# A two-layer decoder on one core: the last batch's causal output, linear cross attention, norm and routing in two parts of 128 queries, with two more expert tiles between them

## The chip, the core and the metric

The kernel runs on one core of one Trainium2 chip. A core has a matrix engine (TensorE, in the profile PE, its weight loads PEld) and four others: VectorE (DVE), ScalarE (ACT), GpSimd (POOL) and SyncE (SP), which here only starts transfers between the chip's main memory and the core's own. Each engine works through its own instructions in the order in which the program gives them, and waits on semaphores for the others and for transfers. Matmul results land in PSUM, which has eight banks. The metric is the time of the whole kernel on the device in microseconds (us).

## The reference

A decoder of two layers, each followed by its norm, in float32: four batches of 256 tokens with 256 channels, and a context of 1601 rows for each batch.

```python
# layer 0                                           16 heads of 16
x = norm(x + sliding_window_attention(x))           # window 64
x = norm(x + attention(q=x, kv=[context, x]))       # one head of 256
x = norm(x + ternary_ffn(x))                        # quantised weights and activations
# layer 1                                           16 heads of 192, 4 of keys
x = norm(x + causal_attention(x))                   # keys and values from a latent of 64, rotary part
x = norm(x + gate(x) * linear_attention(x, context) @ Wo)
x = norm(x + moe(x))                                # 8 experts, the best 2 of each token
```

The linear attention uses a feature map f (x + 1 above zero, exp(x) below), so that a batch needs of its context only the sums f(k) v and f(k) for each head. In the mixture of experts (MoE) a token's two best experts each compute w2(silu(w1 x) * w3 x), and the two are added with the router's weights.

## The kernel before, in words

**The order of work.** No line of the kernel says in which order an engine does its work. The functions of the decoder record operations with what they read and write. The `Loom` (lines 176 to 353) then lays them out like a list scheduler: of all operations that could go next it takes the one that can start first (`weave`, line 301), by a model of costs: a time for each operation on each engine (`Side.cost`, line 386; for matmuls the microseconds given to `piece`, line 240), the delay from one engine to the next (`LAT`, line 182), and a model of the transfers (lines 336 to 338): all of them one after the other at `RATE`, 0.25 MB/us, plus a landing time of 1.6 us. Ties go by a priority (`at_prio`) and the order of recording. What comes out is a fixed program for each engine. At run time the engines wait for real data, in that order. So a change in the model alone can change the order of anything. The profile puts matmuls at L253 (`mm`), transposes on PE at L260 (`turn`), plain transfers at L267, and all work of DVE, ACT and POOL at L382, where it is issued.

**The stages.** Layer 0's sliding-window attention (`l0_attention`, line 652) runs together with the context sums (`context_sums`, line 741; matmuls `wkv,KT` and `kf,V` in the profile, sums kvs) from 0 to about 130 us. It loads xt (a batch's x transposed), the weights wqkv, and for each batch the context KT and V in pieces of up to 1 MB, all through SP's one queue. Batches share two buffers of v (`vs[b % 2]`). A softmax is a maximum (`nm`) on DVE, four exponentials on ACT with their sums, a reciprocal (`rs`) on DVE, and a scaling on DVE or POOL; then PE transposes the result (`ident,at`). `l1_weights` (line 1002) multiplies layer 1's weights into each other; `kr<-wkr,trig` is its first step on DVE and needs the transfers wkr and trig. Layer 0's cross attention, the FFN, and layer 1's attention follow.

**The end.** For each batch b the main loop (lines 1464 to 1475) records layer 1's causal attention (`l1_attention`, line 1052: four groups of four heads, `four`, line 1069; in each first queries 0 to 127 against 128 keys, then queries 128 to 255 against 256, then `P·V` for all of them, `aTa,ctk` and `aTb,ctk`; the output projection w2o in two halves), `l1_cross` (line 1126: qf and the gate by `xt,wqg`, `kvs,qf`, the division that gives o, `wxo`), the norm (`norm`, line 602: statistics on DVE, a power on POOL for rstd, transposes on PE), and `route` (line 1227). `route` writes x to two arrays in main memory, xd and acc, and enters each token with its weight into the list of each of its two experts: four indirect transfers on POOL (`enter`, line 1212). A tile is 128 rows of one expert's list. `tile_table` (line 1287) works out on DVE which tiles there are. `expert_tile` (line 1337) fetches a tile's list entries (SP), gathers its rows xg from xd (POOL, L1349), transposes them, multiplies by w1 and w3 (`w,xgT`), takes Tanh and two products (ACT, DVE), transposes, multiplies by w2 (`w2e,ehT`), and adds the result ey to acc by an indirect transfer on POOL (L1357). Each of these add-ups waits until the one before has landed. After batch 3's cross attention, ahead of its routing, stand 5 early tiles (`EARLY`) that the tokens of batches 0 to 2 fill for certain; 18 (`LATE`) follow when all is routed. At the very end acc is loaded, normalised and stored.

The transfer model, and the last loop:

```python
            if op.size is not None:
                self.free["DMA"] = max(self.free["DMA"], at + us) + op.size / self.RATE
                op.end, op.engine = self.free["DMA"] + op.land, "DMA"
...
        if b == B - 1:
            at_prio(8)
            tab, taken = tile_table(EARLY, None)
            for i in range(EARLY):
                expert_tile(i, tab)
```

Of the kernel before, what the change touches and what calls it, by code (L numbers as in the profile page):

```python
# [175 lines left out]
class Loom:  # L176
# [62 lines left out]
    @contextmanager  # L239
    def piece(self, us, claims=(), ins=(), what=""):  # L240

        self.cur = ([], [], list(ins))
        yield
        fns, outs, ins = self.cur
        self.cur = None
        self.op({"PE": (us, us, lambda: [f() for f in fns])}, outs, ins, claims, what=what)
# [54 lines left out]
    def weave(self):  # L301
# [11 lines left out]
        while left:  # L313
# [22 lines left out]
            if op.size is not None:  # L336
                self.free["DMA"] = max(self.free["DMA"], at + us) + op.size / self.RATE
                op.end, op.engine = self.free["DMA"] + op.land, "DMA"
# [70 lines left out]
def decoder(ctx: ExitStack, tc: tile.TileContext, a: dict, out: bass.AP):  # L409
# [178 lines left out]
    def normalise(x):  # L588
        mv = tiny((P, 2, 2), "mv")
        for t in range(2):  # L590
            st = tiny((P, 6), "st")
            k.vector.bn_stats(st, x[:, t, :])
            k.vector.bn_aggr(mv[:, t, :], st)
        rstd = tiny((P, 2), "rstd")
        k.gpsimd.tensor_scalar(rstd, mv[:, :, 1], 1e-5, None, ALU.add)
        k.gpsimd.tensor_tensor(rstd, rstd, mhalf, ALU.pow)
        for t in range(2):
            k.vector.tensor_scalar(
                x[:, t, :], x[:, t, :], mv[:, t, 0:1], rstd[:, t : t + 1], ALU.subtract, ALU.mult
            )  # L600

    def norm(b, x):

        normalise(x)
        xt = xpool.tile((P, 2, S), F32, "xt")
        ps = bank((P, 2, 2, P))
        for t in range(2):
            with piece(0.22, [xt], what="norm"):
                for c in range(2):
                    turn(ps[:, c, t, :], x[:, t, c * P : (c + 1) * P], ident)  # L610
        evac(xt.rearrange("p c (t q) -> p c t q", t=2), ps)
        X[b], XT[b] = x, xt
# [12 lines left out]
    def project_out(pool, x_new, t, x_old, o, wo, gate=None):  # L625
# [6 lines left out]
        if gate is None:  # L632
            evac(oT, pt)
        else:
            k.vector.scalar_tensor_tensor(oT, gate[:, :, t * P : (t + 1) * P], 1.0, pt, ALU.add, ALU.mult)
# [16 lines left out]
    def l0_attention(b):  # L652
# [11 lines left out]
        for i in range(3):  # L664
            pv = bank((P, D))
            with piece(0.86, what="v"):
                for c in range(2):
                    mm(pv, XT[b][:, c, 64 * i : 64 * i + P], wqkv[:, c, 2 * D :], c == 0, c == 1)
# [65 lines left out]
    def feature_map(pool, dst, ps, n, width, bufs=2):  # L734

        e = pool.tile((P, 512), F32, "fm", bufs=bufs)[:n, :width]
        k.scalar.activation(e, ps, AF.Exp)
# [314 lines left out]
    def l1_attention(b):  # L1052
# [16 lines left out]
        def four(q4):  # L1069

            ps = project_in(XT[b], lambda c, j: m_w[:, c, 2 * q4 + j, :], [qeT], "q")
            evac(qeT[:, 2 * q4 : 2 * q4 + 2, :], ps)
            aT0 = pool.tile((P, 2, 2, S), F32, "aTa")
            aT1 = pool.tile((P, 2, 2, P), F32, "aTb")
            for t in range(2):
# [4 lines left out]
                with piece(0.65 if t == 0 else 1.15, [at, aT0, aT1], what="scores"):  # L1080
# [15 lines left out]
                for kc in range(t + 1):  # L1096
# [4 lines left out]
                    dst = aT0[:, :, :, t * P : (t + 1) * P] if kc == 0 else aT1  # L1101
                    evac(dst, pt.rearrange("p (u i) q -> p u i q", u=2))

            po = bank((P, 2, S))
            with piece(1.42, what="pv"):
                for u in range(2):
                    half = slice(64 * u, 64 * u + 64)
                    mm(po[half], ctk[:, 0, :], aT0[:, u], True, False, skip_group_check=True)
                for u in range(2):
                    half = slice(64 * u, 64 * u + 64)  # L1110
                    mm(po[half, :, P:], ctk[:, 1, :], aT1[:, u], False, True, skip_group_check=True)
            evac(qeT[:, 2 * q4 : 2 * q4 + 2, :], po)

        for q4 in range(4):
            four(q4)
        xn = new_x()
        for t in range(2):
            py = bank((P, D))
            with piece(3.46, [xn], what="out"):
                for i in range(8):  # L1120
                    mm(py, qeT[:, i, t * P : (t + 1) * P], w2o[:, i, :], i == 0, i == 7)
            k.vector.tensor_tensor(xn[:, t, :], py, X[b][:, t, :], ALU.add)
        norm(b, xn)


    def l1_cross(b):
        pool = p5
        qf = pool.tile((P, 2, S), F32, "qf", bufs=1)
        pq = project_in(XT[b], lambda c, j: wqg[:, 0, c, j * P : (j + 1) * P], [qf], "q")
        feature_map(pool, qf.rearrange("p j q -> p (j q)"), pq.rearrange("p j q -> p (j q)"), P, 512, 1)  # L1130

        gate = pool.tile((P, 2, S), F32, "gate", bufs=1)
        pg = project_in(XT[b], lambda c, j: wqg[:, 1, c, j * P : (j + 1) * P], [gate], "gate")
        for j in range(2):
            k.scalar.activation(gate[:, j], pg[:, j], AF.Tanh, bias=bg[:, j : j + 1], scale=0.5)
        xn = new_x()
        for t in range(2):
            pn = bank((P, H, 17))
            o = pool.tile((P, H, 16), F32, "o")
            with piece(0.47, [o], what="kvs"):  # L1140
                for j in range(2):
                    mm(
                        pn[:, 8 * j : 8 * j + 8, :].rearrange("p h e -> p (h e)"),
                        qf[:, j, t * P : (t + 1) * P],
# [9 lines left out]
            project_out(pool, xn, t, X[b], o.rearrange("p h e -> p (h e)"), wxo, gate)  # L1154
        norm(b, xn)
# [8 lines left out]
    EARLY = -(-(2 * 3 * S - NE * (P - 1)) // P)  # L1164
    LATE = 2 * T // P + NE - 1 - EARLY
# [61 lines left out]
    def route(b):  # L1227
        pool = p5
        tokens, ahead, onesb, _, _, nxt = state
        for d in (xd, acc):  # L1230
            k.dma_start(d[b * S : (b + 1) * S, :].rearrange("(t p) d -> p t d", p=P), X[b])
        entry = pool.tile((P, 2, 2, 2), I32, "entry", bufs=B)
        k.vector.tensor_copy(
            entry[:, :, :, 1], tokens[:, 2 * b : 2 * b + 2].unsqueeze(2).to_broadcast([P, 2, 2])
        )
        pl = bank((P, 2, NE))
        with piece(0.83, what="route"):
            for t in range(2):
                for c in range(2):
                    mm(pl[:, t, :], XT[b][:, c, t * P : (t + 1) * P], wg[:, c, :], c == 0, c == 1)  # L1240

        lg = tiny((P, 2, NE), "lg")
        k.scalar.activation(lg, pl, AF.Tanh, scale=1.0 / 30.0)
        k.scalar.activation(lg, lg, AF.Exp, scale=30.0)
        m = tiny((P, 2), "lm")
        k.vector.reduce_sum(m, lg, axis=AX.X)
        k.vector.reciprocal(m, m)
        k.vector.tensor_tensor(lg, lg, m.unsqueeze(2).to_broadcast([P, 2, NE]), ALU.mult)
        top = tiny((P, 2, 8), "top")
        ix = tiny((P, 2, 8), "ix", U32)  # L1250
        for t in range(2):

            k.vector.max(top[:, t, :], lg[:, t, :])
            k.vector.max_index(ix[:, t, :], top[:, t, :], lg[:, t, :])
        ixf = tiny((P, 2, 2), "ixf")
        k.vector.tensor_copy(ixf, ix[:, :, 0:2])
        hot = tiny((P, 2, 2, NE), "hot")
        k.vector.tensor_tensor(
            hot,
            iota8.unsqueeze(1).unsqueeze(1).to_broadcast([P, 2, 2, NE]),  # L1260
            ixf.unsqueeze(3).to_broadcast([P, 2, 2, NE]),
            ALU.is_equal,
        )
        hotb = tiny((P, 2, NE), "hotb", BF16)
# [3 lines left out]
        pr = bank((P, 3, NE))  # L1268
        with piece(0.3, what="rank"):
            mm(pr[:, 0, :], ahead, hotb[:, 0, :], True, True)  # L1270
            mm(pr[:, 1, :], onesb, hotb[:, 0, :], True, False)
            mm(pr[:, 1, :], ahead, hotb[:, 1, :], False, True)
            mm(pr[:, 2, :], onesb, hotb[:, 0, :], True, False)
            mm(pr[:, 2, :], onesb, hotb[:, 1, :], False, True)
        at = tiny((P, 2, 1, NE), "place")
        k.vector.tensor_tensor(at[:, :, 0, :], pr[:, :2, :], nxt.unsqueeze(1).to_broadcast([P, 2, NE]), ALU.add)
        k.vector.tensor_tensor(nxt, nxt, pr[:, 2, :], ALU.add)
        k.vector.tensor_tensor(hot, hot, at.to_broadcast([P, 2, 2, NE]), ALU.mult)
        row = tiny((P, 2, 2), "row")
        k.vector.reduce_sum(row, hot, axis=AX.X)  # L1280
        rowi = tiny((P, 2, 2), "rowi", I32)
        k.vector.tensor_copy(rowi, row)
        for t in range(2):
            for e in range(2):
                enter(rowi[:, t, e : e + 1], entry[:, t, e, :])

    def tile_table(n, taken):


        iotaN, start, nxt = state[3:]  # L1290

        def some(w, tag):
            return p5.tile((P, w), F32, f"{tag}{n}", bufs=1)

        nt = some(NE, "nt")
        k.vector.tensor_scalar(
            nt, nxt, 1.0 / P, -127.0 / 256.0 if taken is None else 127.0 / 256.0, ALU.mult, ALU.add
        )
        k.vector.tensor_scalar(nt, nt, MAGIC, MAGIC, ALU.add, ALU.subtract)
        st = start  # L1300
        if taken is not None:
            st = some(NE + 1, "st")
            k.vector.tensor_copy(st, start)
            k.vector.tensor_tensor(st[:, :NE], st[:, :NE], taken, ALU.add)
# [9 lines left out]
        past = p5.tile((P, n, NE), F32, f"past{n}", bufs=1)  # L1314
# [11 lines left out]
        tab = p5.tile((P, 2, n), I32, f"tab{n}", bufs=1)  # L1326
        k.vector.tensor_scalar(tab[:, 0, :], ex, float(NE - 1), None, ALU.min)
        k.vector.tensor_scalar(tab[:, 1, :], row, float(P), None, ALU.mult)
        if taken is None:

            taken = some(NE, "taken")
            k.vector.tensor_tensor(taken, nt, upto, ALU.subtract)
            k.vector.tensor_scalar(taken, taken, float(n), 0.0, ALU.add, ALU.max)
            k.vector.tensor_tensor(taken, taken, nt, ALU.min)
        return tab, taken

    def expert_tile(i, tab):
# [70 lines left out]
        k.op({"POOL": (1.65, 1.65, add_up)}, [acc], [y, ids], size=0.13, what="add up")  # L1408
# [43 lines left out]
    state = moe_prepare()  # L1452
# [11 lines left out]
    for b in range(B):  # L1464
        at_prio(7, b)
        l1_attention(b)
# [90 lines left out]
```

## Time and profile before

| | |
|---|---|
| time, median of 3 runs | 734.64 us (733.61 to 734.69) |
| profiled execution: time, span | 731.26 us, 729.5 us |
| granted clock of PE, mean over the span | 0.979 |
| PE busy | 672.8 us, 92% |
| DVE, ACT, POOL busy | 438.5 (60%), 302.6 (41%), 158.3 (22%) us |
| bytes moved | 63.39 MB, mean 87 GB/s |

The span is the profiled execution's time from its first to its last instruction; its own time is 1.76 us longer. The profile cuts the span into 40 slices, and gives each engine's busy share of a slice in tenths. `PEclk` is the share of PE's full clock that was granted. A line of the timeline gives the start, the time and the engine of instructions of one kind in a row, their line, what they write and read, how many they were, and in brackets how long the engine stood idle before them and what it waited for. A line of the windows gives, for a stretch, its length, then PE, PEld, DVE, ACT and POOL busy with their instruction counts, then the granted clock, the share of the DMA engines and GB/s. A line on a transfer ends with its size and the time from issue to landing. A float32 matmul shows as two instructions of PE (24 for twelve), a transpose as one.

### The profile page before, as it was taken

To read this page: it belongs to the slowest core of one execution; us is meant where nothing else is said; L and a number is where in the kernel's file an instruction comes from. 1 tells how busy PE (TensorE), PEld (TensorE's weight loads), DVE (VectorE), ACT (ScalarE), POOL (GpSimd) and SP (SyncE) were. 2 spreads that over 40 slices of the span, in tenths; PEclk is the share of its full clock that TensorE was granted. 3 is DMA by queue.
4 is the path that set the end of the run, shared out by engine and by line. 5 is a ranking of instruction groups with operands and counts; after the bars stand their busy time and mean duration, and the time that the engine had idled before them with its cause. 6 is when DMAs were issued, how large, how long until landed. Compare 5 with 4: busy or idle time off the path is not lost.

```text
span 729.5 us, 11204 instructions
## 1 busy us (share of the span) xinstructions
PE 672.8 (92%) x3920; PEld 490.8 (67%) x3920; DVE 438.5 (60%) x1067; ACT 302.6 (41%) x931; POOL 158.3 (22%) x190
## 2 busy tenths in 40 slices
PE   7999999999999999999899999999977959999970
PEld 5778787678867786767676777777654635665640
DVE  4899886334493535665999877887754513333323
ACT  2868664211232224343467765656611202222210
POOL 3220324022100000000121010303122456522232
PEclk9999999999999999999999999999999989999995
DMA  9901212538632230000203900003601143312214
GB/s 307 341 18 59 92 35 87 173 128 273 219 115 91 91 122 1 1 0 1 53 1 115 347 1 30 1 30 62 199 2 37 30 56 90 59 21 23 23 22 123
DMA packets 51819, 63.39 MB, mean 87 GB/s; under 512 B 7758, under 2 KB 41684, under 8 KB 51764
## 3 DMA queue, kind: packets, MB, share of 16 engines
q1 hardware_dynamic: 46836, 56.63, 23.9%
q0 software_dynamic: 4928, 6.05, 5.3%
q8 instruction: 32, 0.52, 0.3%
q14 instruction: 23, 0.19, 0.1%
HBM read 54.05 MB, written 8.61 MB: 86 GB/s over the span
## 4 chain that ended last, share of the span: by engine, by line
PE 73%; DVE 13%; DMA 5%; ACT 4%; issue 2%; POOL 1%; SPq 0%; POOLq 0%; DVEq 0%; ACTq 0%
PE bank L253 65%; PE bank L260 8%; DVE at L382 3%; ACT at L382 3%; DMA acc<-ey,mine 2%; DVE nm L382 2%; DVE x L382 2%; DVE h L382 1%; DVE as L382 1%; DMA lists<-entry,rowi 1%; DMA xg<-xd,mine 1%; DVE st L382 1%; DMA x<-acc 1%; POOL rstd L382 1%; DMA wqkv<-in_wqkvT 0%
## 5 line engine op out<-in xcount | busy, mean ns | idle before, releaser
L382 ACT ACTIVATE at<-at,nm 128x128 f32<-128x128 f32 (+1 forms) x256 | 106.3, 418 | 23.5 <-DVE nm L382 22.9
L253 PE MATMUL bank<-w,xgT 128*128 x184 | 85.0, 608 | 0.5 <-ACT xgT L382 0.5
L260 PE MATMUL bank<-ident,at 128*128 128x128 f32 (+1 forms) x440 | 60.4, 275 | 1.1 <-DVE at L382 0.4
L253 PEld LDWEIGHTS bank<-w,xgT 128*128 128x128 f32 x184 | 35.0, 197 | 37.1 <-issue 36.0
L260 PEld LDWEIGHTS bank<-ident,at 128*128 128x128 f32 (+1 forms) x440 | 50.7, 141 | 13.0 <-issue 4.8
L382 POOL TENSOR_SCALAR rstd<-mv 128x2 f32<-128x2 f32 x24 | 6.3, 263 | 244.2 <-DVE mv L382 226.1
L253 PE MATMUL bank<-V,aT 128*128 128x256 f32 (+1 forms) x240 | 55.2, 380 | 1.4 <-DVE o L382 1.4
L253 PE MATMUL bank<-KT,qT 128*128 128x512 f32 (+1 forms) x128 | 53.8, 554 | 0.0
L253 PEld LDWEIGHTS bank<-V,aT 128*128 128x128 f32 (+1 forms) x240 | 45.0, 190 | 11.6 <-issue 4.4
L1357 POOL DMA_INDIRECT acc<-ey,mine x23 | 36.1, 1569 | 72.7 <-DVE ey L382 42.1
L253 PE MATMUL bank<-kf,V 128*128 128x256 f32 (+1 forms) x208 | 49.9, 382 | 1.1 <-DVE kf L382 1.1
L382 DVE TENSOR_REDUCE nm<-at 128x4 f32<-128x512 f32 x64 | 50.7, 809 | 0.5
L253 PE MATMUL bank<-wkv,KT 128*128 128x256 f32 (+1 forms) x208 | 49.7, 383 | 0.0
L382 ACT ACTIVATION_READ_ACCUMULATOR at<-at,nm 128x1 f32 x256 | 48.4, 189 | 0.0
L253 PE MATMUL bank<-w2e,ehT 128*128 x184 | 43.9, 385 | 2.9 <-ACT ehT L382 2.8
L382 POOL TENSOR_TENSOR at<-at,rs 128x512 f32<-128x512 f32 (+1 forms) x17 | 20.3, 1191 | 111.0 <-DVE rs L382 70.0
L253 PEld LDWEIGHTS bank<-kf,V 128*128 128x128 f32 (+1 forms) x208 | 38.5, 190 | 7.7 <-DVE kf L382 2.3
L382 ACT COPY aT<-bank 128x512 f32<-128x512 f32 (+2 forms) x57 | 29.1, 540 | 33.3 <-PE bank L260 33.0
L253 PEld LDWEIGHTS bank<-wkv,KT 128*128 128x128 f32 (+1 forms) x208 | 37.7, 186 | 7.5 <-issue 1.9
L253 PEld LDWEIGHTS bank<-w2e,ehT 128*128 128x128 f32 x184 | 34.0, 190 | 12.3 <-ACT ehT L382 4.4
L382 DVE TENSOR_TENSOR at<-at,rs 128x512 f32<-128x512 f32 (+1 forms) x47 | 39.2, 834 | 1.0
L382 ACT ACTIVATE eh<-bank 128x512 f32<-128x512 f32 x23 | 13.7, 597 | 59.4 <-PE bank L253 59.4
(248 smaller groups left out, 1252.0 us busy)
## 6 DMA issues: line engine op xcount, KB each, us to landing
w<-in_w SPq DMA_DIRECT2D x16, 512.0 KB, 9.3
KT<-in_ctxT SPq DMA_DIRECT2D x6, 1024.0 KB, 6.2
V<-in_ctx SPq DMA_DIRECT2D x6, 1024.0 KB, 7.5
w2e<-in_w SPq DMA_DIRECT2D x8, 512.0 KB, 9.4
KT<-in_ctxT SPq DMA_DIRECT2D x6, 577.0 KB, 4.7
V<-in_ctx SPq DMA_DIRECT2D x6, 512.0 KB, 4.1
wq<-in_w1qT SPq DMA_DIRECT2D x8, 256.0 KB, 4.8
wo<-in_w1o SPq DMA_DIRECT2D x8, 256.0 KB, 3.1
```

The costliest lines, as they stand in the source:

```text
L253: lambda: self.nc.tensor.matmul(real(o), real(lhsT), real(rhs), start=real(start), stop=stop, **kw)
L260: fns.append(lambda: self.nc.tensor.transpose(real(o), real(x), real(ident)))
L382: return getattr(engine, method)(*[real(x) for x in args], **{k: real(x) for k, x in kw.items()})
L1357: nc.gpsimd.indirect_dma_start(out=acc.real(), out_offset=bass.IndirectOffsetOnAxis(ap=ids.real(), axis=0), in_=y.real(), in_offset=None, ...
```

## The change

`l1_attention` becomes a generator. For batch 3 it does `four` for queries 0 to 127 in all four groups, with the four projections of q by m_w and P·V of 128 columns, then the output projection and norm of that half, and yields; then the same for queries 128 to 255. The other batches do both halves of a group together as before. `l1_cross`, `norm` and `route` take a list `ts` of halves. So batch 3's linear attention, norm and routing run once for each half, with matmuls of 128 columns instead of 256. The early tiles become 5 after the first half's cross attention and 2 after the second's (those that 896 routed tokens fill for certain), and 16 remain: 23 as before. There are three tile tables instead of two.

Three edits are to the planner. In its model a transfer under 0.3 MB passes larger ones that are queued ahead of it. An add-up's landing time is 2.9 instead of 1.6 us. And the matmuls of v in `l0_attention` wait in the plan until the last reads of that buffer of v are planned (`over`).

```diff
-    def piece(self, us, claims=(), ins=(), what=""):
+    def piece(self, us, claims=(), ins=(), over=(), what=""):
...
+        read = [o for v in over for _, o in v.buf.reads]
+        self.op({"PE": (us, us, lambda: [f() for f in fns])}, outs, ins, claims, after=read, what=what)
...
             if op.size is not None:
-                self.free["DMA"] = max(self.free["DMA"], at + us) + op.size / self.RATE
-                op.end, op.engine = self.free["DMA"] + op.land, "DMA"
+                begin, took = at + us, op.size / self.RATE
+                self.free["DMA"] = max(self.free["DMA"], begin) + took
+                if op.size < 0.3:
+                    behind = self.free["DMA"] - took > begin
+                    op.end = min(self.free["DMA"], begin + (2 * took + 1.0 if behind else took)) + op.land
+                else:
+                    op.end = self.free["DMA"] + op.land
+                op.engine = "DMA"
...
-            with piece(0.86, what="v"):
+            with piece(0.86, over=[v], what="v"):
...
-        def four(q4):
-            ps = project_in(XT[b], lambda c, j: m_w[:, c, 2 * q4 + j, :], [qeT], "q")
-            evac(qeT[:, 2 * q4 : 2 * q4 + 2, :], ps)
+        def four(q4, ts):
+            pair = slice(2 * q4, 2 * q4 + 2)
+            if ts[0] == 0:
+                ps = project_in(XT[b], lambda c, j: m_w[:, c, 2 * q4 + j, :], [qeT], "q")
+                evac(qeT[:, pair, :], ps)
...
-    EARLY = -(-(2 * 3 * S - NE * (P - 1)) // P)
-    LATE = 2 * T // P + NE - 1 - EARLY
+    EARLY = [-(-(2 * n - NE * (P - 1)) // P) for n in (3 * S, T - P)]
+    EARLY[1] -= EARLY[0]
+    LATE = 2 * T // P + NE - 1 - sum(EARLY)
...
-    def route(b):
+    def route(b, ts, x, xt):
...
-        k.op({"POOL": (1.65, 1.65, add_up)}, [acc], [y, ids], size=0.13, what="add up")
+        k.op({"POOL": (1.65, 1.65, add_up)}, [acc], [y, ids], size=0.13, land=2.9, what="add up")
...
-        l1_attention(b)
-        at_prio(6, b)
-        l1_cross(b)
-        if b == B - 1:
-            at_prio(8)
-            tab, taken = tile_table(EARLY, None)
-            for i in range(EARLY):
-                expert_tile(i, tab)
-        at_prio(6, b)
-        route(b)
+        for ts, x, xt in l1_attention(b):
+            at_prio(6, b)
+            if ts[0] == 0:
+                xn, xnt = new_x(), new_xt()
+            l1_cross(b, ts, x, xt, xn, xnt)
+            if b == B - 1:
+                at_prio(8)
+                n = EARLY[ts[0]]
+                tab, taken = tile_table(n, taken)
+                for i in range(n):
+                    expert_tile(i, tab)
+            at_prio(6, b)
+            route(b, ts, xn, xnt)
+            at_prio(7, b)
```

## The prediction

> **What bounds the kernel now.** I read the forty slices first, then TensorE's (PE) timeline at both ends of the run, and last the queues that feed those ends.
>
> ```profile
> ## 2 busy tenths in 40 slices
> PE   7999999999999999999899999999977959999970
> PEclk9999999999999999999999999999999989999995
> ```
>
> A slice is 18.2 us. PE is full from the second slice to the 29th (one 8 among them), and the chain of waits puts 73% of the span on it. The holes are the first slice, those between 529 and 602 us, and the end. In the middle the window from 40 to 60 us is the rule: PE is busy 19.95 of 20 us, so **time lost ahead of 40 us is never made up**.
>
> ```profile
> 40.00:60.00 20.00, 19.95 (x208) 16.38 (x200) 19.91 (x45) 15.81 (x71) 4.43 (x5) 1.00 0.00 1
> ```
>
> PE's timeline over the late holes, with the idle time before a line and its releaser in brackets:
>
> ```profile
> 541.24 0.67 PE L260 MATMUL bank<-ident,x 128*128 128x128 f32 x4 [3.16 <-DVE x L382]
> 542.58 5.29 PE L253 MATMUL bank<-xt,wqg 128*128 128x256 f32 x16 [0.67 <-ACT xt L382]
> 550.67 0.41 PE L260 MATMUL bank<-ident,xg 128*128 128x128 f32 x2 [2.80 <-DMA xg<-xd,mine]
> ...
> 553.72 4.74 PE L253 MATMUL bank<-w,xgT 128*128 x8
> ...
> 569.17 3.60 PE L253 MATMUL bank<-w,xgT 128*128 x8
> ...
> 596.45 0.66 PE L260 MATMUL bank<-ident,xg 128*128 128x128 f32 x2 [7.54 <-DMA xg<-xd,mine]
> ```
>
> Batch 3 goes through causal attention, norm, linear attention, norm and routing as one chain, with only 5 early tiles (23 in all) to lay beside it: it waits for its own norm (3.16) and for the first gathered rows (2.80). The longest wait, 7.54, comes from POOL: its add-up at 591.48 waits 5.14 for the previous add-up, and the gathers stand behind it.
>
> ```profile
> 591.48 1.56 POOL L1357 DMA_INDIRECT acc<-ey,mine  x1 [5.14 <-DMA acc<-ey,mine]
> 710.20 1.55 POOL L1357 DMA_INDIRECT acc<-ey,mine  x1 [2.91 <-DMA acc<-ey,mine]
> ```
>
> **The change, first place: the end.** I count from 501.6 us, where batch 2's output projection ends. Before, PE's idle from there to 597.6 is 0.31 + 1.26 + 0.22 + 0.69 + 3.16 + 0.67 + 2.80 + 0.90 + 0.35 + 0.68 + 7.54 + 0.46 = 19.0, and in the last 40 us some 2.8 more (0.66, 0.73, 0.73 and small ones): 21.8. After a hole the same matmuls run slower: wqg 5.29 against 3.72 at 507.60, kvs 1.68 against 1.19 at 512.93, the tiles' first eight 4.74 and, after the 7.54, 5.08 against 3.60. That is 1.57 + 0.49 + 1.14 + 1.48 = 4.7. The last add-up is ready at 708.6 (its ey) and goes at 710.20: 1.6. Together 28.1 us that better cover could win.
>
> In the changed order I laid every instruction of PE, DVE, ACT and POOL down with the durations of these rows (four transposes .44, scores .65 and 1.06, wxo .87, w2o 3.46 a half, a tile 5.86, norm about 3 us of DVE and POOL). Part 1's norm, projections and routing now lie beside the scores and softmaxes of part 2, and part 1's list entries and gathers ahead of part 2's norm. What stays before the first early tile: .35 (a late aT copy), 1.2 (norm of batch 2), 1.45 (first turn of part 1), .75, 2.95 (kvs of part 1: DVE does the maximum of the fourth softmax before o), .9 and .3 (part 1's wxo and its norm), 2.4 (part 2's norm), .7, and about 1.4 in kvs: 12.4. From there tiles, two more than before, lie beside part 2's routing; the late lists are asked for early enough (first late rows at 589, needed at 592), and POOL's order has the gathers ahead of the blocked add-ups, so the 7.54 goes. Each hand-over there has a hop of .1 to .3 that I didn't lay down: 1.5. Slow matmuls after the two holes over 2.4: 2.5, with 1.1 and 1.5 of before as the rows. The last tile stands alone, where before the last two were paired: 1.7, and its add-up waits for none. More PE work: sixteen wqg matmuls of 128 columns at .26 for eight of .445, .6; P·V as .53 and 1.06 for 1.44, four times, .6; a fourth m_w ahead of part 1, .7. Sum 12.4 + 1.5 + 2.5 + 1.7 + 1.9 = 20.0 for 28.1: **-8**.
>
> Neither end of that is shown by the trace. If part 2's matmuls fill nearly all the waits, it is -15 (12.4 goes to 5); if DVE, which is busy 14.90 of 20 us from 520 to 540 already and gets the third table (some 25 small operations of .17) and more, smaller vector work, is late at each hand-over by .4, it is -4. The split loads cost nothing: route's transfers to xd and acc become two each on SP, which has no other work there; the split norm and the halves of `entry` add issue slots on POOL, hidden behind its 4 to 8 us waits for DVE.
>
> **Second place: the start.** The diff touches the planner too: transfers under 0.3 MB are now modelled as passing the large ones queued ahead. The program's order is laid out by that model, so the first 130 us are reshuffled though no operation there changes. (Its two smaller edits, the longer landing of an add-up and v's matmuls waiting for the last reads of v, act through that order alone, which I walked.) PE today:
>
> ```profile
> 13.63 1.33 PE L253 MATMUL bank<-kT,qT 32*128 32x256 f32 x24
> 14.89 5.45 PE L253 MATMUL bank<-wkv,KT 128*128 128x256 f32 x24
> 21.47 1.99 PE L253 MATMUL bank<-kf,V 128*128 128x256 f32 x8 [1.13 <-DVE kf L382]
> ```
>
> In the new order batch 1's q, k and v stand behind the scores of 13.63, ahead of any wkv,KT. They need batch 1's xt. SP's issue order at the start is the same, so its rows hold:
>
> ```profile
> 10.85 1.04 SPq L267 DMA_DIRECT2D wkv<-in_w1kvT  x1
> 11.93 0.71 SPq L267 DMA_DIRECT2D xt<-in_xT  x1
> ...
> 25.32 0.43 SPq L267 DMA_DIRECT2D trig<-in_rope  x1
> ```
>
> and the landings that the trace has, in KB and us from issue:
>
> ```profile
> w0o<-in_w0oT SPq DMA_DIRECT2D x1, 256.0 KB, 8.0
> wkv<-in_w1kvT SPq DMA_DIRECT2D x1, 256.0 KB, 8.1
> ...
> V<-in_ctx SPq DMA_DIRECT2D x1, 1024.0 KB, 9.5
> ...
> wvdecT<-in_w1vdecT SPq DMA_DIRECT2D x1, 128.0 KB, 8.4
> ```
>
> w0o, issued 10.34, lands 18.34, and wkv behind it 18.95: in the order of issue, .61 for 256 KB. So xt lands at about 19.6, and PE idles from 14.9 to 19.6: 4.7.
>
> The second wait is DVE's. `kr<-wkr,trig` moves from 48.41 to right behind batch 1's v copies, ahead of the reciprocals of the third and fourth softmax:
>
> ```profile
> 48.41 1.04 DVE L382 TENSOR_TENSOR kr<-wkr,trig 128x512 f32<-128x512 f32 x1
> ```
>
> It waits for trig, 8 KB, behind V (18.98 + 9.5 = 28.5) and ahead of wvdecT (26.27 + 8.4 = 34.7, with 256 KB between, so about 34.1). In DVE's queue stand those reciprocals, for them POOL's scaling (1.04) and for that PE's transposes. From 34.1: kr 1.0, reciprocal .2, scaling 1.0, transposes twice .44 with hops: PE goes on with wkv,KT at 37.3. The same PE work (what today is done by 26.9, less 1.8 of wkv,KT, 2.0 of kf,V and 1.5 of scores, plus 6.5 of q, k and v) stands today at 28.1. Lag 9.2, plus 1 of slow matmuls after the hole, less .45 that PE idles today up to 42 us: **+10**. Bounds: with trig at 28.5 the first wait of 4.7 stays and some 3 of the second, +8; with ACT late too (batch 1's kT copy stands ahead of the first sixteen exponentials and waits for xt) +13.
>
> The Trainium skill speaks against the planner's new assumption. "DMA: Bandwidth & Descriptors", section Queues, rings and completion order, says that each DMA engine takes descriptors in the order of its ring, though completions may cross. The 8.0 and 8.1 us of two neighbours agree; by it xt waits for wkv, without it the start costs little. "TensorE: Matmul & The Clock Gate", Part 1: The HAM clock gate, halves the clock after an idle window of about 3.4 us; by an estimate from it the hole at 14.9 would cost up to 1.7 more. The trace shows 5.08 for 3.60.
>
> **Sum.** +10 - 8 = +2. Against the profiled execution (span 729.5, 731.26 in all, 1.76 around the span) that is 733.1; the median of the runs is 734.64, so **736.5**.
>
> **Rivals.**
> (A) As worked out, +2, with -2 to +5 from the two bounds together: chance .47.
> (B) *Faster: the late hand-overs close.* In the part from 501.6 on, part 2's four groups are independent of part 1's norm and routing, and fill 12.4 down to 5: -15 + 10 = -5, 729.5. It decides as soon as the end wins over 10. For it: 7.54, 3.16 and 2.80 are single waits with clear causes. Against: DVE does both parts' vector work in a fixed order. Chance .23.
> (C) *The end gives little.* DVE late at each hand-over, -4, + 10 = +6, 740.5. For it: 14.90 of 20 busy. Against: today's large waits are of DMAs, not DVE. Chance .24.
> (D) *The planner is right:* small transfers do pass; xt is there at 15, trig by 28; the start costs about 2: -6, 728.5. Against: the landings above. Chance .06.
>
> That the change does nothing is excluded: the orders differ on every engine.
>
> **Numbers.** A measurement of this kernel tells about 0.2%, 1.5 us, from no change. Faster: .06 of A, .22 of B, .05 of D: .33. Within: .16 of A, .01 of B, .01 of D: .18. Slower: .25 of A, all .24 of C: .49. Range: B and the gentler start (-15 + 8 = -7) give 727.5, C with the harder start (-4 + 13 = +9) 743.6; I take 727 to 744. A alone: 732.5 to 739.5.
>
> **What would show it.** At the start: an idle of about 4.7 before the second `xt,wqkv` at about 19.6, kr at about 34 with PE idle behind it, and PE at 60 to 300 us some 10 us behind today's rows. At the end: no wait over 5 us for xg between 560 and 610; idle before the first early tile near 12; the last add-up without a wait. It is wrong if xt or trig is there when PE and DVE ask, or if waits at the end add up to far less or more than 12.4.

## The result, and the profile after

The changed kernel takes 733.49 us (median of 12 runs, 731.82 to 735.13), the kernel before 733.69 us (12 runs, 731.76 to 734.89): a ratio of 0.9997, with an interval of 0.9985 to 1.001. A second comparison (e9 below) gave 1.0016 (1.0003 to 1.0029), 1.2 us more. So the change does nothing or loses about 1 us, less than 0.3%, where 1.9 us more had been forecast. The profiled executions differ by more, with spans of 732.2 us and 729.5: that of the kernel before (731.26 us in all) was shorter than each of its 12 runs, that of the changed kernel (733.92) was near its median.

Behind the nothing stand two large amounts. A mark that stands at the same place of both programs separates them: PE's first `wgate,xt`, the routing of layer 1's batch 0. Before, it starts at 448.68 us and 280.8 us of the span follow; after, at 460.20 with 272.0 to follow. **The start lost 11.5 us, the end won 8.8.** These are single executions; a second one of the changed kernel (e9) has 458.9 and 271.0, so about 1 us of each is scatter.

The forty slices of the changed kernel:

```profile
PE   4899899999999999999899999999978999999970
PEclk9799999999999999999999999999998999999995
```

The first slice falls from 7 to 4, the second and the fifth from 9 to 8, and the granted clock of the second from 9 to 7; at the other end the slices with a 7, a 7 and a 5 have become a 7 and an 8. PE's timeline at the start:

```profile
12.64 1.33 PE L255 MATMUL bank<-kT,qT 32*128 32x256 f32 x24
19.02 6.63 PE L255 MATMUL bank<-xt,wqkv 128*128 128x256 f32 x16 [5.05 <-DMA xt<-in_xT]
...
30.68 1.89 PE L255 MATMUL bank<-wkv,KT 128*128 128x256 f32 x8
34.62 1.73 PE L262 MATMUL bank<-ident,at 128*128 128x128 f32 x8 [2.04 <-POOL at L391]
36.14 3.13 PE L255 MATMUL bank<-wkv,KT 128*128 128x256 f32 x8
```

and the two instructions on ACT and DVE that stand behind them:

```profile
22.82 0.69 ACT L391 ACTIVATE kT<-bank,qmask 128x512 f32<-128x512 f32 x1 [9.48 <-PE bank L255]
```

```profile
32.31 0.69 DVE L391 TENSOR_TENSOR kr<-wkr,trig 128x512 f32<-128x512 f32 x1 [3.64 <-DMA trig<-in_rope]
```

PE waits 5.05 for batch 1's xt; the same 16 instructions took 3.72 before and take 6.63 after the hole. ACT's sixteen exponentials stand behind kT and begin 6 us later than before (23.40 for 17.42). Then DVE waits for trig, and PE for what comes behind that. At the end, PE's waits of over half a microsecond from 530 to 700 us are now these (two more, 0.79 and 0.73, stand in the last tile):

```profile
534.80 0.63 PE L262 MATMUL bank<-ident,at 128*128 128x128 f32 x4 [0.64 <-DVE at L391]
...
549.13 0.41 PE L262 MATMUL bank<-ident,o 128*128 128x128 f32 x2 [2.66 <-DVE o L391]
550.26 0.75 PE L262 MATMUL bank<-ident,at 128*128 128x128 f32 x4 [0.72 <-ACT at L391]
...
563.13 0.41 PE L262 MATMUL bank<-ident,x 128*128 128x128 f32 x2 [2.34 <-DVE ixf L391]
...
569.25 0.30 PE L262 MATMUL bank<-ident,o 128*128 128x128 f32 x1 [0.60 <-DVE past L391]
...
585.74 0.41 PE L262 MATMUL bank<-ident,x 128*128 128x128 f32 x2 [0.87 <-DVE x L391]
```

None is for gathered rows. The sum of PE's idle from 480 to 620 us is 11.2, where the kernel before has 19.7.

### The profile page after: what moved, and what is told of

It reads as the page before. It is cut to its first block, busy times and chain, and to the rows that moved or that the text cites. A ratio compares the mean times of both kernels' runs of the same rounds, so it can differ in the third digit from the quotient of the medians.

```text
span 732.2 us, 11343 instructions
## 1 busy us (share of the span) xinstructions
PE 677.0 (92%) x3947; PEld 495.5 (68%) x3951; DVE 443.2 (61%) x1106; ACT 307.0 (42%) x943; POOL 161.0 (22%) x195
## 4 chain that ended last, share of the span: by engine, by line
PE 73%; DVE 14%; DMA 5%; SPq 2%; issue 2%; POOL 1%; ACT 1%; POOLq 0%; DVEq 0%; ACTq 0%
PE bank L255 64%; PE bank L262 9%; DVE at L391 3%; DVE nm L391 2%; SPq L269 2%; DVE x L391 2%; DVE h L391 1%; DMA xt<-in_xT 1%; DMA trig<-in_rope 1%; DMA acc<-ey,mine 1%; DVE as L391 1%; DVE st L391 1%; POOL rstd L391 1%; DMA xg<-xd,mine 1%; DMA x<-acc 1%
## 5 line engine op out<-in xcount | busy, mean ns | idle before, releaser
L255 PE MATMUL bank<-w,xgT 128*128 x184 | 82.5, 593 | 0.3 <-issue 0.3
L262 PE MATMUL bank<-ident,at 128*128 128x128 f32 (+1 forms) x440 | 62.4, 280 | 5.0 <-POOL at L391 2.0
L391 POOL TENSOR_SCALAR rstd<-mv 128x2 f32<-128x2 f32 (+1 forms) x26 | 6.8, 261 | 247.6 <-DVE mv L391 209.9
L255 PEld LDWEIGHTS bank<-V,aT 128*128 128x128 f32 (+1 forms) x240 | 45.2, 190 | 10.9 <-issue 3.3
L255 PE MATMUL bank<-wkv,KT 128*128 128x256 f32 (+1 forms) x208 | 51.2, 389 | 0.0
L391 DVE TENSOR_REDUCE nm<-at 128x4 f32<-128x512 f32 (+1 forms) x64 | 50.5, 810 | 0.5
L391 DVE TENSOR_TENSOR at<-at,rs 128x512 f32<-128x512 f32 (+1 forms) x46 | 41.5, 905 | 0.8
L255 PEld LDWEIGHTS bank<-w2e,ehT 128*128 128x128 f32 x184 | 34.1, 190 | 11.3 <-issue 4.3
```

What stands on the lines that cost most here:

```text
L255: lambda: self.nc.tensor.matmul(real(o), real(lhsT), real(rhs), start=real(start), stop=stop, **kw)
L262: fns.append(lambda: self.nc.tensor.transpose(real(o), real(x), real(ident)))
L391: return getattr(engine, method)(*[real(x) for x in args], **{k: real(x) for k, x in kw.items()})
```

## The experiments

The theory was that of the prediction: the planner's new order of the start costs some 10 us, the split and its two tiles win nearly as much. Its first rival was that a lag at the start is made good where the end waits anyway, so that neither part moves much. In the table, mark is the start of the first `wgate,xt` and rest what follows of the span, both from one profiled execution; the ratio is to the kernel before on the same chip. The expected times below stem from the first comparison, where the kernel before took 733.7 us; beside e1 to e4 it took 731.46, so 2.2 us are to be added to their times before the two are compared.

| | mark, us | rest, us | ratio (interval) |
|---|---|---|---|
| before | 448.7 | 280.8 | |
| changed | 460.2 | 272.0 | 0.9997 (0.9985 to 1.001) |
| e1 planner's model alone | 460.8 | 281.3 | 1.0162 (1.0137 to 1.0188) |
| e2 split alone | 448.8 | 271.1 | 0.9863 (0.9841 to 0.9885) |
| e3 add-up's landing alone | 448.4 | 280.0 | 0.9985 (0.9972 to 0.9998) |
| e4 split, no tiles between | 448.4 | 277.6 | 0.9961 (0.9947 to 0.9974) |
| e5 changed, trig early | 456.8 | 281.1 | 1.0033 (1.0005 to 1.0061) |
| e6 changed, xt early | 461.1 | 280.3 | 1.0107 (1.0078 to 1.0137) |
| e7 changed, both early | 449.4 | 277.0 | 0.9932 (0.9908 to 0.9956) |
| e8 changed, model after 140 us | 449.9 | 277.6 | 0.9955 (0.9933 to 0.9977) |
| e9 changed | 458.9 | 271.0 | 1.0016 (1.0003 to 1.0029) |
| e10 split alone | 448.0 | 271.1 | 0.9855 (0.9836 to 0.9874) |
| e11 changed, both early | 449.6 | 270.7 | 0.9870 (0.9854 to 0.9887) |
| e12 e10 with the old landing | 448.3 | 271.9 | 0.9884 (0.9865 to 0.9902) |

### The two halves apart: e1 and e2

**e1** is the kernel before with the new model of small transfers. It has `over` too; what `over` does without that model at the start is read from e8.

```diff
-                self.free["DMA"] = max(self.free["DMA"], at + us) + op.size / self.RATE
-                op.end, op.engine = self.free["DMA"] + op.land, "DMA"
+                begin, took = at + us, op.size / self.RATE
...
+                if op.size < 0.3:
...
-            with piece(0.86, what="v"):
+            with piece(0.86, over=[v], what="v"):
```

> The kernel before, with the changed model of small transfers and the wait of v's matmuls in the plan; batch 3 stays whole and an add-up's landing time stays 1.6. PE's order up to the end of layer 0's attention is that of the changed kernel. Theory (two large amounts that cancel): the new order of the start costs all that the changed kernel has lost by 140 us, 11 us: 744 to 746 us, PE idle about 5 before the second xt,wqkv and about 2 before the ident,at that waits for kr's successors. Rival (the trace's difference of 11 us at 300 us is made good where the end waits for norms and transfers anyway): 733 to 736 us.

Measured: 1.0162, 11.9 us on 731.46. The two waits are there, and the lag isn't made good, since the end's own waits come from chains that start as late as PE does:

```profile
19.83 6.50 PE L254 MATMUL bank<-xt,wqkv 128*128 128x256 f32 x16 [5.51 <-DMA xt<-in_xT]
...
35.30 1.72 PE L261 MATMUL bank<-ident,at 128*128 128x128 f32 x8 [2.05 <-POOL at L389]
...
608.83 0.66 PE L261 MATMUL bank<-ident,xg 128*128 128x128 f32 x2 [7.88 <-DMA xg<-xd,mine]
```

The long wait for late rows (7.54 at 596.45 before) simply stands 12.4 us later and is as long. The rival is out.

**e2** is the changed kernel with the old model and without `over`; PE's, ACT's, POOL's and DVE's orders up to the last stage are those of before.

```diff
-                if op.size < 0.3:
...
+                self.free["DMA"] = max(self.free["DMA"], at + us) + op.size / self.RATE
+                op.end, op.engine = self.free["DMA"] + op.land, "DMA"
...
-            with piece(0.86, over=[v], what="v"):
+            with piece(0.86, what="v"):
```

> The changed kernel with the old model of transfers and without the wait of v's matmuls in the plan: batch 3 in two parts, three tables, add-up landing 2.9. Its order on PE is that of the kernel before up to the last stage. Theory (two large amounts): the end gains what the changed kernel gains after 11 us of lag, 9 us: 723 to 726 us, idle of PE from 480 to 620 us about 11 where the kernel before has 19.7. Rival (the two parts gain only because a late start leaves other engines time to catch up): 730 to 734 us.

Measured: 721.63 against 731.46, 0.9863, so 9.8 us faster; e10, the same kernel on another chip, 0.9855. Of the runs, +11.9 and -10 make about +2; the changed kernel itself measures -0.2 and +1.2. This version beats both kernels. Its largest waits in batch 3 are those of the changed kernel, 11.4 to 12.7 us earlier:

```profile
537.69 0.41 PE L262 MATMUL bank<-ident,o 128*128 128x128 f32 x2 [2.66 <-DVE o L385]
...
550.39 0.66 PE L262 MATMUL bank<-ident,x 128*128 128x128 f32 x2 [2.34 <-DVE ixf L385]
```

### What wins at the end: e3, e4, e12

**e3**, the add-up's landing time alone, in the kernel before:

```diff
-        k.op({"POOL": (1.65, 1.65, add_up)}, [acc], [y, ids], size=0.13, what="add up")
+        k.op({"POOL": (1.65, 1.65, add_up)}, [acc], [y, ids], size=0.13, land=2.9, what="add up")
```

> The kernel before with nothing but the add-up's landing time of 2.9 in the plan; batch 3 whole, 5 early tiles. Theory A (the split and its two tiles make the gain at the end): 732 to 735 us, a wait of PE over 5 us for xg near 596 stays. Theory B (the order of gathers and add-ups on POOL alone makes most of it): the 7.5 us wait shrinks by 4 to 6 with the slow matmuls behind it, 727 to 730 us.

Measured: 730.38, 1.1 us less, theory A. The long wait stays, only smaller ones behind it go:

```profile
596.09 0.66 PE L260 MATMUL bank<-ident,xg 128*128 128x128 f32 x2 [7.74 <-DMA xg<-xd,mine]
```

PE has run dry at 588.35, and SP fetches the late lists only from 589.04 on, having waited 4.9 for the entries into them, the last of which is issued at 582.94, to land. The edit moves later gathers ahead; the first still stands behind an add-up that waits:

```profile
591.13 1.57 POOL L1357 DMA_INDIRECT acc<-ey,mine  x1 [5.33 <-DMA acc<-ey,mine]
593.00 1.02 POOL L1349 DMA_INDIRECT xg<-xd,mine  x1 [0.30 <-DMA mine<-lists]
```

In e4 the first late gather goes 2.9 us after SP's first fetch (587.39 and 590.29). By an estimate from that, the gather here could have gone at about 591.9, so the blocked add-up is worth some 1 us of the 7.74, and the rest is a wait for the lists. In e2 SP fetches from 587.24 on, and PE has tiles until 596.8.

**e4**, e2 without the two tiles between the parts:

```diff
-    EARLY[1] -= EARLY[0]
+    EARLY[1] = 0
...
-            if b == B - 1:
+            if b == B - 1 and EARLY[ts[0]]:
```

> As e2_split_alone, but without the two tiles between the parts: batch 3 in two parts, 5 early tiles, 18 late ones, two tables. Theory A (the parts cover each other, the two tiles cover the second part's norm and routing): 3 to 6 us above e2_split_alone, 727 to 731 us, with PE waiting for xg before the late tiles. Theory B (the two tiles do nothing, the split does it all): within 1 us of e2_split_alone.

Measured: 728.20, 6.6 us above e2: theory A, slightly more than its bound. The waits in batch 3 are the same, and the one for late rows, 1.10 in e2, is long again:

```profile
593.09 0.44 PE L262 MATMUL bank<-ident,xg 128*128 128x128 f32 x2 [3.66 <-DMA xg<-xd,mine]
593.99 5.10 PE L255 MATMUL bank<-w,xgT 128*128 x8 [0.46 <-ACT xgT L385]
```

That is 2.6 more of this wait, the 0.46 behind it and 1.5 of slow matmuls (5.10 for 3.60): some 4.5 of the 6.6. The rest isn't placed. So of the 10 us about 3 are the split's and the landing time's (1.1 by itself in e3), nearly 7 the two tiles', which only the split makes possible.

**e12**, e2 with the old landing time (the line of e3 turned back):

> e2_split_alone with the add-up's landing time back at 1.6 in the plan. On POOL two add-ups now stand ahead of three gathers of the first late rows. Theory (the landing time matters only where late rows are short, and the split alone shifts the add-ups into that spot): a wait of PE for xg of 3 us or more near 590 to 600 us, 2 to 6 us above e10_split_again. Rival (as in e3_land, where this edit alone gave 1.1 us): within 1.5 us of e10_split_again.

Measured: 722.83 against 720.73 of e10, 2.1 us: the low end of theory, and all five runs (721.79 to 724.24) lie above e10's four (720.63 to 721.20). The wait is there but 1.78 long, not 3:

```profile
598.91 0.44 PE L262 MATMUL bank<-ident,xg 128*128 128x128 f32 x2 [1.78 <-DMA xg<-xd,mine]
```

In their profiled executions e10 has no such wait and e2, the same program, one of 1.10. So the edit costs something, but that it costs it by this wait is not shown.

### What loses at the start: e5, e6, e7, e11

These move loads on SP's queue and leave the order of all computing as in the changed kernel: the traces show the same instructions in the same order on PE, DVE, ACT and POOL. e5 issues trig and wkr early, e6 batch 1's xt, e7 both.

```diff
+    load_x(1)                                      # e6, e7
     KV[2] = load_ctx(2)
...
     for b in range(1, B):
-        load_x(b)
+        if b > 1:                                  # e6, e7
+            load_x(b)
         load_res(b)
+        if b == 1:                                 # e5, e7
+            trig = load(pm, (P, 2, 8), a["rope"], "trig", 1)
+            wkr2 = load(pm, (P, 2, KVH, 64), a["w1krT"], "wkr2", 1)
...
-        wkr2 = load(pool, (P, 2, KVH, 64), a["w1krT"], "wkr2", 1)    # e5, e7
-        trig = load(pool, (P, 2, 8), a["rope"], "trig", 1)           # e5, e7
```

> The changed kernel with one edit: the loads of trig and wkr are issued right behind batch 1's xt and x, ahead of context 0. The order of all computing stays. Theory (the two waits of the start lie in series and the later landing binds): PE's idle before the ident,at at 34.6 us (2.04) goes, with the slow matmuls behind it (some 2): 2 to 4 us below the changed kernel, so at a ratio to the kernel before of 0.994 to 0.997. Rival (the 16 exponentials that wait for batch 1's kT bind, not kr): no change, 0.999 to 1.001.

> The changed kernel with one edit: batch 1's xt is loaded ahead of context 2, so that it is there when PE asks at 14 us. The order of all computing stays. Theory (trig's landing at 32 us sets when PE goes on, whatever came before): the idle of 5 us before the second xt,wqkv goes, but comes back, longer than 2.04, before the ident,at that waits for kr: within 1.5 us of the changed kernel, ratio 0.998 to 1.002. Rival (each wait costs its own length): 6 to 8 us below the changed kernel, ratio 0.988 to 0.992.

> The changed kernel with both edits, batch 1's xt and trig with wkr early. The order of all computing stays. Theory (the planner's new order is no worse in itself, only its transfers are late): the whole loss of the start comes back, 9 to 11 us below the changed kernel, ratio 0.985 to 0.988, as e2_split_alone. Rival (the order itself loses on PE, DVE or ACT besides the two waits): ratio above 0.992.

At the mark the theory holds in all three: -3.4, +0.9 and -10.8 us against the changed kernel. In e5 the second wait is gone:

```profile
31.34 1.89 PE L255 MATMUL bank<-wkv,KT 128*128 128x256 f32 x8
33.07 1.04 PE L262 MATMUL bank<-ident,at 128*128 128x128 f32 x8
```

In e6 the first is gone and all of it is back in the second, since kr still waits for trig and starts at 32.88 (32.31 in the changed kernel):

```profile
14.16 3.72 PE L255 MATMUL bank<-xt,wqkv 128*128 128x256 f32 x16
...
35.19 1.97 PE L262 MATMUL bank<-ident,at 128*128 128x128 f32 x8 [9.96 <-POOL at L391]
```

To remove the first wait alone is worth nothing (0.9 is within the scatter of a mark), the second alone 3.4, both 10.8: they lie in series before one gate.

The ratios were missed, all three upwards, by 0.5 to 0.9%, and e7's 0.9932 is by the letter its rival's. The rest after the mark is 5 to 9 us longer than the changed kernel's 272.0 though its order is the same; e8, run beside them, has it too, and the kernel before took 734.53 us there, the most of the four comparisons. In the executions of e5, e6 and e7 DVE and ACT stand still in the tiles, here e5's:

```profile
624.16 0.69 DVE L391 TENSOR_TENSOR eh<-bank,eh 128x512 f32<-128x512 f32 x1 [3.64 <-remote]
624.31 0.60 ACT L391 ACTIVATE eh<-bank 128x512 f32<-128x512 f32 x1 [4.51 <-remote]
```

**e11**, e7 once more, with **e9** and **e10** on its chip, was to tell whether the new start causes that:

> The changed kernel itself, on the same chip as the next three. Theory: ratio to the kernel before 0.998 to 1.003, as at first; the other three stand to it as the lag of PE at 450 us stands. Rival (the end of every kernel in two parts has lost its gain since): ratio above 1.005.

> e2_split_alone once more, as the measure for e11. Theory: ratio 0.984 to 0.989. Rival (its gain was of one chip): above 0.992.

> e7_both_early once more. There the start stood where theory put it (the last ident,mT at 156.3 us against 167.1 of the changed kernel), but PE, DVE and ACT stood still together for some us near 614 us. Theory (those stalls are no work of the changed start, since the order of the end is the same): within 2.5 us of e10_split_again, ratio 0.986 to 0.991. Rival (the new order of the start costs 4 us or more at the end): ratio above 0.992, with the stall near 614 us again and none in e10_split_again.

Measured: 1.0016, 0.9855 and 0.9870. e11 is 1.2 us above e10, its rest 270.7, and no such standstill is in it. So the standstill is no part of these programs' order, and e7's rival falls. With both loads early, the changed kernel's start costs 1.6 us at the mark (449.6 for 448.0) in place of 10.9 (458.9).

### The rule later on: e8

```diff
-                if op.size < 0.3:
+                if op.size < 0.3 and begin > 140:
```

> The changed kernel with the new rule for small transfers used in the plan only for those issued after 140 us of planned time; v's matmuls still wait in the plan. Theory (the rule harms only at the start, where transfers queue): within 2 us of e2_split_alone, ratio 0.984 to 0.989. Rival (the rule harms all along, or v's wait in the plan does): ratio above 0.992.

Measured: 0.9955, by the letter the rival's. But it ran beside e5 to e7, with a rest of 277.6, the same as e7's 277.0, and its mark is 449.9. It stands 1.2 us above e7 in the median (731.36 and 730.12). The start's 10 us do come back, although `over` stays: the model of small transfers is what cost them, and `over` at most the 1 to 2 us by which this mark lies above those of e2 and e10. Whether the rule costs something after 140 us can't be told from it.

## Why the prediction was right and where it was not

**The time.** 736.5 was given, +1.9 on the median; the measured -0.2 and, on e9's chip, +1.2 are in the range of 727 to 744 and in case A's. Both halves were right in kind; the start was 1.5 to 1.9 us dearer than said and the end won 0.8 to 2.6 more, and that these two nearly cancel is luck. That the likeliest class was "slower" was not borne out: the sum of two terms of 10 was asked to be exact to 1.5, which the terms' own errors don't allow.

**The start, +10: 11.5 in the profile, 11.9 by e1's runs.** Landing of xt: 19.6 said, PE went on at 19.02. kr: 34.1 said, 32.31 measured: trig went out 0.7 earlier than before and took 7.7 us where the sum had 8.8. Third wkv,KT: 37.3 said, 36.14. From today's 28.1 that is a lag of 8.0, and 1.2 of slow matmuls behind (3.13 for 1.89): 9.2 by 40 us. (The first sixteen matmuls behind the hole at 14 us lost 2.9, 6.63 for 3.72, more than the estimate of up to 1.7; it didn't show, because the second wait came after it.) What the sum lacked comes later: three waits that the kernel before doesn't have, the largest of them this:

```profile
88.16 0.76 PE L262 MATMUL bank<-ident,x 128*128 128x128 f32 x4 [1.57 <-DVE x L391]
```

With 0.47 at 85.40 and 0.70 at 118.76 they make 2.7. One of 0.67 that the kernel before has at 221.16 is gone, and 9.2 + 2.7 - 0.7 is 11.2 of the 11.5. I had taken the lag at 40 us to hold because PE was full before; but the order behind it was new as well. e7 has all three (0.47, 1.56 and 0.69) though its transfers are in time, so they belong to the order. The marks of e9, e10 and e11 say the same: 9.3 us go when the transfers are in time, 1.6 stay.

**The end, -8: -8.8 in the profile, -10.0 and -10.6 by the ratios of e2 and e10.** The single waits came as laid down: kvs of part 1 2.66 for 2.95, wxo behind it 0.72 for 0.9, norm of part 2 2.34 for 2.4, norm of batch 2 1.08 for 1.2; the first turn of part 1 only 0.64 and 0.29 for 1.45. Up to the first tile's matmuls PE is idle 9.1 for 12.4, and up to the late tiles 10.0 for 13.9 with the hand-overs, so this term was too large by 3 to 4. The slow matmuls behind the two holes came as said, some 2.6 for 2.5: sixteen wqg took 3.55 behind the 2.34, where eight took 1.14 at 542.60, and the granted clock was 0.72 there (562 to 568 us) and 0.70 behind the 2.66 (549 to 553). The late rows are there in time, but the prediction had the wrong cause for the 7.54 us of before: it put them to the blocked add-up on POOL, which by e3 is worth about 1 us, and what PE lacked were tiles until the lists had come. A second term was wrong: "its add-up waits for none". The last one still waits for its predecessor:

```profile
710.75 0.48 DVE L391 TENSOR_SCALAR ey<-bank,mine 128x256 f32<-128x256 f32 x1 [3.47 <-PE bank L255]
...
712.27 1.54 POOL L1409 DMA_INDIRECT acc<-ey,mine  x1 [2.85 <-DMA acc<-ey,mine]
```

1.0 us from ey to issue, where before it was 1.6: 0.5 won, not 1.6. With 3.9 less idle and 1.1 less won here the sum of -8 becomes -10.9, near what e2 and e10 show.

**The rivals.** B (12.4 closed down to 5) fell, since 9.1 remain; its amount came close, as the end won about the 10 from which it was to decide. C (DVE late at each hand-over) fell, most were a little shorter than said. D (small transfers pass large ones) fell: e1's waits, and wkv issued at 10.30 took 8.0 us, xt behind it at 11.09 some 7.9 until PE ran.

## What to carry to other kernels

When a planner or a cost model is edited together with the kernel, the edit reaches every stage: compare the engines' orders from the first instruction on, and time the two halves apart, since here +11.9 and -10 looked like a change that does nothing. Where two waits lie in series before one instruction, removing the earlier one is worth nothing by itself (here 0.9 us later at the mark, within its scatter); price them by what opens the gate last. Work that fills a hole exactly where lists and gathers are on their way (here two tiles, 7 us) can be worth more than the reordering that makes room for it.

## What the runs showed of the hardware that was not expected

- Against what the changed planner assumes, the small transfer did not pass. The 8 KB of trig, issued at 24.64 us behind large ones on the same queue, let their reader go at 32.31: 7.7 us, as long as the 256 KB of xt (11.09 to 19.02).
- In the profiled executions of e5, e6 and e7, on one chip, DVE and ACT stood still for 3 to 4.5 us at a time among the tiles, with no releaser on the core in the profile ("remote"). The same program (e7 and e11) had none on another chip: a rest of 277.0 and 270.7 us. What it was stays open.
